# Row sums of two attention layers turned by DMA through DRAM instead of on TensorE

## The chip, the cores and the metric

The kernel runs on one core of a Trainium2 chip. A core has five engines with a queue of instructions each: TensorE (PE, matrix products and transposes, results in PSUM), VectorE (DVE), ScalarE (ACT), GpSimd (POOL) and SyncE (SP, which here does nothing but issue DMAs). POOL issues DMAs too. All DMAs of the core run on the same 16 DMA engines. Engines run in parallel, each in its own order, and wait for each other through semaphores. The metric is the device time of one execution in microseconds (us); lower is better.

## What is computed

32 graphs of 512 nodes with 256 features go through four attention layers that share one adjacency matrix (about 6% edges, self edges included). Every layer is followed by a residual sum and a normalisation of each node. Cut to the two layers that the change concerns:

```python
# layer 0: eight heads of 32 features, q.k scores
qkv = einsum('fnc,ck->fnk', x, w_qkv)
scores = einsum('fnhd,fmhd->fhnm', q, k) / sqrt(32)
attn = softmax(where(adj > 0, scores, -1e9), axis=-1)
t = einsum('fhnm,fmhd->fnhd', attn, v).reshape(F, N, C)
x = layernorm(x + t, g1, b1)
x = layernorm(x + relu(x @ w1 + b1_) @ w2 + b2_, g2, b2)

# layer 3: four heads of 64 features, additive scores
q = (h @ W).reshape(B, N, 4, 64)
e = e_src[:, :, None, :] + e_dst[:, None, :, :]
e = where(e >= 0, e, 0.2 * e)
attn = softmax(where(adj > 0, e, -9e15), axis=2)
out = elu(einsum('bijh,bjhd->bihd', attn, q))
```

Layers 1 and 2 are single-head attention with other scores. After each layer comes `x = layernorm(x + layer(x))`.

## The kernel before

**Tiling.** A graph's 512 nodes are four chunks (NC = 4) of 128 partitions; the 256 features are two chunks (KC = 2). All numbers are float32. Exponentials of scores are held transposed: in a tile `p` the partitions are the attended nodes m, the free axis the attending nodes n. The softmax is not normalised there: the product of exponentials and values and the sum of exponentials are formed apart, and the product is divided at the end.

**Layers 0 and 3.** For layer 0, `exps` forms scores of four heads at once on four row groups of PE (L1034) and ACT takes exponentials (L1038). DVE masks with the adjacency matrix (L1086, one operation of 128x2048). PE multiplies by the values into `oT`, features by nodes (L1093). The sums over m are also taken with DMAs: POOL issues accumulating DMAs `p<-p` (`add_dma`, L972), which add up the tiles of four chunks; SP joins two halves (L1112); then four products with a picking matrix (L1065, in `sums`) leave the sums of the eight heads in a PSUM bank, one row of 512 nodes per head, at partitions 32j and 32j + 1. In layer 3, DVE builds the exponentials as a maximum of two products (L1290) and masks them (L1297), PE multiplies by the values (L1306) and takes the sums of four heads (L1281), at partitions 32j. For the last graph (`at_once`) PE takes all sums itself and no accumulating DMA is used.

**The step that changes** is in `sums_back`, `rinv0` and `rinv3`. The sums lie with nodes along the free axis; they are wanted with nodes on partitions. ACT copies the bank to a tile `e` (`evac`, L890), PE transposes its four 128x128 blocks with the identity (L985), and DVE takes reciprocals of the few useful columns straight from PSUM (L994 for layer 0, L1002 for layer 3) into a small tile `ri`. `heads_out` transposes `oT` back, nodes on partitions, in two groups of four (L1017), and DVE scales each group by the reciprocals (L1020). In layer 0 two range checks of the reciprocals follow (L1045, L1046).

**Order.** There is no fixed loop order in the program. Every step is handed to a planner (`plan(engine, ns, run, reads, writes, ...)`) with an engine, a duration, what it reads and writes, and a `lag`: time after the issue of a DMA until its data are taken to have landed. The planner (`place`) walks a model of time and puts the instructions of up to six graphs (WAYS) into each engine's queue by due times. A due time is PACE times the number of the graph plus a place in a table (TENTHS, with tables of their own for the first graphs, FIRST, and the last, LAST); START holds the first graphs back, and EARLY says how far ahead of its due time a step may be placed. On the chip the queues run in the order so made; the waits are on real events. So a step whose true duration differs from the planner's makes its engine wait, or leaves slack.

**Buffers** are of fixed kinds (KINDS): 8 PSUM banks, 8 tiles `p`, 4 tiles `e`, 3 tiles `ri` and others. A step that needs a buffer is placed when one is free.

**SP's queue** holds, for each graph, the load of x (L1347), the store of the result (L1354), the half sum of layer 0 (L1112), and for the additive layers 1 and 3 a row through DRAM: `row<-gT` (L1186) writes it and L1192 reads it back to all partitions, as tile `G`, on which DVE's L1211 and L1290 depend.

Of the kernel before, what the change touches and what calls it, by code (L numbers as in the profile page):

```python
# [9 lines left out]
FP = mybir.dt.float32  # L10
# [7 lines left out]
P = 128  # L18
# [8 lines left out]
H0, H3 = 8, 4  # L27


WAYS = 6  # L30
PACE = 81.87
STAY = 0.00
START = (0, 10.17, 59.24, 97.18, 85.64)
EARLY = 186.52

TENTHS = (0, 35.72, 65.32, 68.92, 152.58, 202.32, 246.27, 266.73, 356.34, 362.66, 490.49)
FIRST = (
    (0, 35.72, 65.32, 62.35, 138.44, 202.98, 246.27, 266.73, 356.34, 362.66, 490.49),
    (-28.44, 35.72, 73.98, 55.02, 197, 202.32, 246.27, 266.73, 356.34, 362.66, 490.49),
    (-31.13, 30.72, 65.32, 68.92, 152.58, 202.32, 246.27, 266.73, 356.34, 362.66, 490.49),  # L40
    (0, 35.77, 65.37, 68.97, 152.63, 202.32, 246.27, 266.73, 356.34, 362.66, 490.49),)
LAST = (
    (0, 35.72, 65.32, 68.92, 152.58, 202.32, 246.27, 266.73, 354.73, 363.36, 490.49),
    (0, 35.72, 65.32, 68.92, 152.58, 202.32, 246.27, 266.73, 356.34, 362.66, 490.49),
    (0, 35.72, 65.32, 68.92, 152.58, 202.26, 246.21, 266.73, 356.34, 412.91, 557.81),
    (-0.21, 35.51, 65.11, 68.71, 152.37, 202.11, 226.96, 232.14, 316.44, 341.17, 500.04),
    (-6.23, 29.49, 59.09, 8.93, 61.49, 76.67, 155.18, 191.54, 257.43, 316.36, 394.47),)
@with_exitstack
def general_path(
    ctx: ExitStack,  # L50
# [387 lines left out]
PE, DVE, ACT, POOL, SP, DMA = "PE", "DVE", "ACT", "POOL", "SP", "DMA"  # L438
# [191 lines left out]
def fast_path(  # L630
# [34 lines left out]
    nc = tc.nc  # L665
    B, N, C = x.shape
    NC = N // P
    KC = C // P
# [4 lines left out]
    dram = ctx.enter_context(tc.tile_pool(name="dram", bufs=1, space=DRAM))  # L673
# [4 lines left out]
        "x": (6, [P, NC, C]), "y": (7, [P, NC, C]), "v": (3, [P, NC, C + 2 * H3]),  # L678
        "t": (9, [P, KC, N]), "p": (8, [P, 4, N]), "e": (4, [P, N]),
        "st": (6, [P, NC, 6]), "mv": (6, [P, NC, 2]), "rs": (18, [P, NC]),  # L680
        "e1": (6, [P, NC * H3]), "gs": (2, [P, NC * H3]), "ri": (3, [P, NC * H0]),
        "gT": (2, [NC * H3, P]),
    }
    buffers = {kind: [const.tile(shape, FP, name=f"{kind}_{i}") for i in range(n)]
               for kind, (n, shape) in KINDS.items()}
    buffers["bank"] = [psum.tile([P, N], FP, name=f"bank_{i}") for i in range(8)]
    buffers["row"] = [dram.tile([NC * H3, P], FP, name=f"row_{i}") for i in range(4)]


    nc.scalar.preload_act_table_set("natural_log_exp_and_others")  # L690
    ident = const.tile([P, P], FP, name="ident")
# [21 lines left out]
    plan = Plan({kind: len(tiles) for kind, tiles in buffers.items()})  # L713
# [7 lines left out]
    def T(slot):  # L721
        return slot.tile if slot.kind is None else buffers[slot.kind][slot.index]
# [4 lines left out]
    def dve(ns, run, reads, writes, port=False):  # L727
        plan(DVE, ns, run, reads, writes, port)
# [159 lines left out]
    def evac(dst, to, src, frm, n, writes):  # L888

        act(170 + n * 0.84, lambda: nc.scalar.activation(to(T(dst)), frm(T(src)), AF.Copy),  # L890
            [src], writes)
# [83 lines left out]
        plan(POOL, 950, run, reads, [dst, started])  # L975
        plan(DMA, 5600 if src else 2650, None, reads + [started], [dst], lag=2500)

    def sums_back(sm):

        sT, bank = Slot("e"), Slot("bank")  # L980
        evac(sT, lambda t: t, sm, lambda b: b, N, [sT])

        def run():
            for c in range(NC):
                nc.tensor.transpose(T(bank)[:, c * P:(c + 1) * P],  # L985
                                    T(sT)[:, c * P:(c + 1) * P], ident)
        plan(PE, 440, run, [sT], [bank])
        return bank

    def rinv0(sm):  # L990


        bank, rinv = sums_back(sm), Slot("ri")
        dve(360, lambda: nc.vector.reciprocal(  # L994
            T(rinv)[:, :NC * H0].rearrange("p (c g j) -> p c g j", c=NC, g=KC),
            T(bank).rearrange("p (c j r) -> p c r j", c=NC, j=4)[:, :, 0:KC, :]), [bank], [rinv])
        return rinv

    def rinv3(sm):

        bank, rinv = sums_back(sm), Slot("ri")
        dve(250, lambda: nc.vector.reciprocal(  # L1002
            T(rinv)[:, :NC * H3], T(bank).rearrange("p (s r) -> p s r", r=32)[:, :, 0]),
            [bank], [rinv])
        return rinv

    def heads_out(oT, rinv, heads):
# [45 lines left out]
    def layer0(xs, at_once):  # L1053
# [7 lines left out]
        oT, sm, totals = Slot("t"), Slot("bank"), []  # L1061
# [19 lines left out]
        for g in range(KC):  # L1081
            av, ps = Slot("bank"), []
            for m in range(NC):
                p = Slot("p")
# [21 lines left out]
        else:  # L1106
# [5 lines left out]
            plan(SP, 450, lambda: nc.sync.dma_start(T(low)[64:], T(high)[64:]), totals, [low, started])  # L1112
            plan(DMA, 1300, None, totals + [started], [low], lag=2500)
            plan(PE, 870, lambda: sums(2, low, True, True), [low], [sm], tiling=2)
        rinv = rinv0(sm)
        t = heads_out(oT, rinv, H0)

        dve(370, lambda: within(T(rinv)[:, :NC * H0], R_MIN, R_MAX), [rinv], [], True)
# [12 lines left out]
        for d in range(KC):  # L1131
            bank = Slot("bank")
# [8 lines left out]
        f = Slot("y")  # L1141
        for c0 in range(0, NC, 2):
            bank = Slot("bank")
# [129 lines left out]
    def layer3(xs, at_once):  # L1273
        xT = transposed(xs)
        totals = []
        q, G, oT, sm = Slot("v"), Slot("p"), Slot("t"), Slot("bank")
        project(xT, l3w, 0, C + 2 * H3, q)
        e1, e02 = gates(q, H3, G)

        def sums(h, p, part, start, stop):  # L1280
            nc.tensor.matmul(T(sm)[32 * h:32 * h + 32, :], pick[:, 0, :], T(p)[:, part, :],  # L1281
                             start=start, stop=stop)
        for k in range(KC):
            av = Slot("bank")
            for m0 in range(0, NC, 2):
                p = Slot("p")
                for m in range(2):
                    for i in range(2):
                        def run(p=p, m=m, i=i, h=2 * k + i, r=(m0 + m) * H3 + 2 * k + i):
                            nc.vector.tensor_scalar(T(p)[:, 2 * m + i, :], T(G)[:, h, :],  # L1290
                                                    T(e1)[:, r:r + 1], T(e02)[:, r:r + 1],
                                                    ALU.mult, ALU.max)
                        dve(560, run, [G, e1, e02], [(p, 2 * m + i)], True)

                def masked(p=p, m0=m0):
                    p4 = T(p).rearrange("p (m h) n -> p m h n", m=2)
                    nc.vector.tensor_tensor(  # L1297
                        p4, p4, T(edge_t)[:, m0:m0 + 2, :].unsqueeze(2).to_broadcast([P, 2, 2, N]),
                        ALU.mult)
                dve(2300, masked, [p, edge_t], [p], True)  # L1300

                def run(p=p, m0=m0, k=k, av=av):
                    for m in range(2):
                        for i in range(2):
                            h = 2 * k + i
                            nc.tensor.matmul(T(av)[i * D3:(i + 1) * D3, :],  # L1306
                                             T(q)[:, m0 + m, 2 * H3 + h * D3:2 * H3 + (h + 1) * D3],
                                             T(p)[:, 2 * m + i, :], start=(m0 + m == 0),
                                             stop=(m0 + m == NC - 1))
                plan(PE, 1770, run, [q, p], [av], tiling=3)  # L1310
                if at_once:
                    plan(PE, 1740, lambda p=p, k=k, m0=m0: [sums(
                        2 * k + i, p, 2 * m + i, m0 + m == 0, m0 + m == NC - 1)
                        for m in range(2) for i in range(2)], [p], [sm], tiling=2)
                    skip(2 if m0 else 0)
                elif m0 == 0:
                    total = p
                else:
                    add_dma(total, p)
                    add_dma(total, None)  # L1320
                    totals.append(total)
            evac(oT, lambda t, k=k: t[:, k, :], av, lambda b: b, N, [(oT, k)])
        if at_once:
            skip(1)
        else:
            plan(PE, 870, lambda: [sums(h, totals[h // 2], h % 2, True, True) for h in range(H3)],
                 totals, [sm], tiling=2)
        t = heads_out(oT, rinv3(sm), H3)

        e, y = Slot("y"), Slot("y")  # L1330
        for c0 in range(0, NC, 2):
            w, parts = slice(c0, c0 + 2), (c0, c0 + 1)
            act(600, lambda w=w: nc.scalar.activation(T(e)[:, w, :], T(t)[:, w, :], AF.Exp),
                [(t, c) for c in parts], [(e, c) for c in parts])
            act(600, lambda w=w: nc.scalar.activation(T(y)[:, w, :], T(t)[:, w, :], AF.Relu),
                [(t, c) for c in parts], [(y, c) for c in parts])
            add(y, y, xs, c0)
            dve(790, lambda w=w: nc.vector.scalar_tensor_tensor(
                T(y)[:, w, :], T(e)[:, w, :], 1.0, T(y)[:, w, :], ALU.min, ALU.add),
                [(s, c) for s in (y, e) for c in parts], [(y, c) for c in parts], True)  # L1340
        return y
# [95 lines left out]
```

## Time and profile before

| | |
|---|---|
| Median of 3 runs | 2897.5 us (2895.68 to 2899.0) |
| Profiled execution: time, span | 2893.58 us, 2891.7 us |
| PE clock granted | 0.993 |
| Chain that ended last | PE 92%, DVE 3%, DMA 2% of the span |
| DMA queues, share of 16 engines' span | POOL's p<-p 57.2%, SP's 11.6% |
| DVE masking of layer 0, L1086 | 256 operations, 618.2 us |
| PE output transposes L1017 | 512, 68.8 us |

The page counts, for each engine, the time in which an instruction of it ran. The share is an average: filling and draining of the pipeline of graphs are in it. In a line of a group, the numbers are the count, the busy time, the mean of one in ns, and after the last bar the idle time of the engine ahead of these instructions and what ended it. A matrix product in float32 appears as two records of PE, a transpose as one. DMA packets are counted one by one with their size.

### The profile page before, as it was taken

What the parts mean: (1) busy time and instruction counts of PE and PEld (TensorE: products, weight loads), DVE (VectorE), ACT (ScalarE), POOL (GpSimd) and SP (SyncE); (2) the same over time, 40 slices, a digit from 0 to 9 for tenths busy, and PEclk for the clock granted to TensorE, in tenths of its full rate; (3) what the DMA queues carried; (4) which work ended last, traced back from release to release, by engine and by line L of the source; (5) the groups of instructions that cost most, each with busy time, mean ns of one, the idle gap of its engine ahead of it and who ended that gap; (6) DMA issues with size and microseconds to landing.
All of it is one profiled execution on the core that took longest, in us unless ns stands there. A gap on an engine that the chain in (4) does not pass through costs nothing.

```text
span 2891.7 us, 39629 instructions
## 1 busy us (share of the span) xinstructions
PE 2832.4 (98%) x14014; PEld 1579.2 (55%) x14014; DVE 2443.2 (84%) x4076; ACT 1885.5 (65%) x4104; POOL 865.9 (30%) x962
## 2 busy tenths in 40 slices
PE   8899999999999999999999999999999999999996
PEld 3355555555555555555555555555555555554562
DVE  5568888888888988888988888988888888888877
ACT  4566667666667666666666666666676666676553
POOL 1233333232333232332232333232333323333312
PEclk9999999999999999999999999999999999999998
DMA  6856777777777777777777777776776777775125
GB/s 168 169 110 142 150 159 164 154 144 160 145 161 153 159 149 158 149 160 157 147 152 150 157 157 155 152 160 144 162 157 150 155 153 146 161 163 115 35 55 132
DMA packets 101149, 424.44 MB, mean 147 GB/s; under 512 B 10256, under 2 KB 46224, under 8 KB 59152
## 3 DMA queue, kind: packets, MB, share of 16 engines
q0 software_dynamic: 49600, 325.08, 57.2%
q1 hardware_dynamic: 51344, 96.75, 11.6%
q8 instruction: 113, 1.85, 0.2%
q14 instruction: 92, 0.75, 0.1%
HBM read 63.38 MB, written 17.10 MB: 28 GB/s over the span
## 4 chain that ended last, share of the span: by engine, by line
PE 92%; DVE 3%; DMA 2%; issue 1%; ACT 1%; POOL 0%; SPq 0%; ACTq 0%; DVEq 0%; POOLq 0%
PE bank L929 15%; PE bank L915 11%; PE bank L1034 9%; PE bank L1093 8%; PE bank L1306 8%; PE bank L1221 7%; PE bank L1244 7%; PE bank L1260 7%; PE bank L902 5%; PE bank L1136 4%; PE bank L1148 4%; PE bank L1017 2%; DMA p<-p 1%; PE bank L1281 1%; PE bank L1065 1%
## 5 line engine op out<-in xcount | busy, mean ns | idle before, releaser
L972 POOL DMA_DIRECT2D p<-p x372 | 322.3, 871 | 1787.8 <-DMA p<-p 568.4
L1086 DVE TENSOR_TENSOR p<-p,edge_t 128x2048 f32<-128x2048 f32 x256 | 618.2, 2424 | 59.7 <-ACT p L1038 59.5
L890 ACT ACTIVATE t<-bank 128x512 f32<-128x512 f32 x640 | 373.5, 596 | 384.2 <-PE bank L915 125.4
L1038 ACT ACTIVATE p<-bank 128x512 f32<-128x512 f32 x1024 | 537.9, 599 | 89.2 <-PE bank L1034 87.6
L943 DVE BATCH_NORM_STATS2 st<-y 128x6 f32<-128x256 f32 x768 | 315.9, 411 | 35.6 <-POOL y L960 26.0
L1290 DVE TENSOR_SCALAR p<-p,e,e 128x512 f32<-128x512 f32 x512 | 331.3, 680 | 1.0 <-DMA p<-row 1.0
L960 POOL TENSOR_TENSOR y<-y,x 128x512 f32<-128x512 f32 x192 | 273.7, 1432 | 158.2 <-ACT y L1265 100.1
L1297 DVE TENSOR_TENSOR p<-p,edge_t 128x2048 f32<-128x2048 f32 x128 | 304.9, 2382 | 2.2
L1034 PE MATMUL bank<-t,t 32*128 32x512 f32 x2048 | 302.6, 644 | 0.0
L953 ACT ACTIVATE x<-y,rs,rs 128x256 f32<-128x256 f32 x512 | 277.6, 596 | 24.6 <-DVE rs L950 24.3
L1093 PE MATMUL bank<-p,v 128*32 128x512 f32 x2048 | 275.2, 609 | 12.5 <-DVE p L1086 9.7
L1306 PE MATMUL bank<-p,v 128*64 128x512 f32 x1024 | 242.8, 605 | 3.6 <-DVE p L1297 3.6
L915 PE MATMUL bank<-t,wqkv 128*128 128x512 f32 x512 | 241.6, 595 | 0.7 <-ACT t L890 0.7
L1221 PE MATMUL bank<-v,p 128*128 128x257 f32 x1024 | 237.8, 381 | 0.7 <-DVE p L1214 0.4
L890 ACT ACTIVATE v<-bank 128x264 f32<-128x264 f32 (+2 forms) x384 | 176.5, 460 | 90.2 <-PE bank L929 88.3
L1260 PE MATMUL bank<-v,p 128*128 128x257 f32 x1024 | 227.4, 380 | 0.0
L1244 PE MATMUL bank<-t,t 128*128 128x512 f32 x512 | 225.1, 592 | 0.0
L1221 PEld LDWEIGHTS bank<-v,p 128*128 128x128 f32 x1024 | 189.5, 190 | 40.3 <-issue 16.3
L1260 PEld LDWEIGHTS bank<-v,p 128*128 128x128 f32 x1024 | 194.2, 190 | 28.6 <-issue 1.3
L1034 PEld LDWEIGHTS bank<-t,t 32*128 32x128 f32 x2048 | 86.0, 184 | 169.5 <-issue 101.5
L944 DVE BATCH_NORM_AGGREGATE mv<-st 128x2 f32<-128x6 f32 x768 | 139.7, 182 | 26.3
L902 PE MATMUL bank<-ident,x 128*128 128x128 f32 x1024 | 148.9, 279 | 11.7 <-DMA x<-in_x_dram 7.7
(121 smaller groups left out, 4148.8 us busy)
## 6 DMA issues: line engine op xcount, KB each, us to landing
p<-p POOLq DMA_DIRECT2D x248, 1024.0 KB, 7.2
p<-p POOLq DMA_DIRECT2D x124, 512.0 KB, 5.7
p<-row SPq DMA_DIRECT2D x32, 1024.0 KB
x<-in_x_dram SPq DMA_DIRECT2D x32, 512.0 KB
out_dram<-x SPq DMA_DIRECT2D x32, 512.0 KB
p<-p SPq DMA_DIRECT2D x31, 512.0 KB
e<-row SPq DMA_DIRECT2D x32, 256.0 KB
t<-in_adj_dram SPq DMA_DIRECT2D x4, 256.0 KB
```

What stands on the lines that cost most here:

```text
L890: act(170 + n * 0.84, lambda: nc.scalar.activation(to(T(dst)), frm(T(src)), AF.Copy), [src], writes)
L915: nc.tensor.matmul(T(bank), T(w)[:, i, col:col + P], T(xT)[:, i, :], start=(i == 0), stop=(i == KC - 1))
L929: nc.tensor.matmul(T(bank)[:, j * width:(j + 1) * width], T(xT)[:, k, (c0 + j) * P:(c0 + j + 1) * P], T(w)[:, k, col:col + width], start=( ...
L1034: nc.tensor.matmul(T(banks[j]), T(kT)[r, g, m * P:(m + 1) * P], T(qT)[r, g, :], start=True, stop=True)
L1038: act(600, lambda j=j: nc.scalar.activation(T(p)[:, j, :], T(banks[j]), AF.Exp, scale=1.0 / math.sqrt(D0)), [banks[j]], [(p, j)])
L1086: dve(2420, lambda p=p, m=m: nc.vector.tensor_tensor(T(p), T(p), T(edge_t)[:, m, :].unsqueeze(1).to_broadcast([P, J, N]), ALU.mult), [p, ( ...
L1093: nc.tensor.matmul(T(av)[j * D0:(j + 1) * D0, :], T(v)[:, m, h * D0:(h + 1) * D0], T(p)[:, j, :], start=(m == 0), stop=(m == NC - 1))
L1221: nc.tensor.matmul(T(bank)[:, :C + 1], T(p)[:, m, c * P:(c + 1) * P], T(v)[:, m, 2:C + 3], start=(m == 0), stop=(m == NC - 1))
L1244: nc.tensor.matmul(T(bank), T(xT)[:, k, m * P:(m + 1) * P], T(qT)[:, k, :], start=(k == 0), stop=(k == KC - 1))
L1260: nc.tensor.matmul(T(bank)[:, :C + 1], T(p)[:, m, c * P:(c + 1) * P], T(v)[:, m, :C + 1], start=(m == 0), stop=(m == NC - 1))
L1290: nc.vector.tensor_scalar(T(p)[:, 2 * m + i, :], T(G)[:, h, :], T(e1)[:, r:r + 1], T(e02)[:, r:r + 1], ALU.mult, ALU.max)
L1306: nc.tensor.matmul(T(av)[i * D3:(i + 1) * D3, :], T(q)[:, m0 + m, 2 * H3 + h * D3:2 * H3 + (h + 1) * D3], T(p)[:, 2 * m + i, :], start=(m0 ...
```

## The change

The transposes on PE are replaced by a way through DRAM. A new function `rinv_of` serves both layers. After the same copy on ACT, four DMAs on SP write the useful rows (two per j in layer 0, one in layer 3) to a DRAM buffer `line`, 2 KB each row. When all four have landed, one more DMA on SP reads the buffer so that nodes lie on partitions: element (h, c, p) goes to partition p, column (h, c). Runs in DRAM and in SBUF do not match in that access, so it moves in pieces of 4 bytes, 4096 of them in layer 0 and 2048 in layer 3. DVE then takes reciprocals from this tile, reordered to what `heads_out` reads. The planner's numbers for the new steps are 450 ns for each issue, and lags of 2000 ns for a write and 3500 ns for the read. A fourth `ri` tile and four `line` buffers are added. The constants of the due times are others (PACE, START, EARLY and the three tables).

```diff
-PACE = 81.87
+PACE = 83.15
-START = (0, 10.17, 59.24, 97.18, 85.64)
-EARLY = 186.52
+START = (0, 11.15, 69.71, 99.02, 152.63)
+EARLY = 180.50
...
-    def sums_back(sm):
-        sT, bank = Slot("e"), Slot("bank")
-        evac(sT, lambda t: t, sm, lambda b: b, N, [sT])
-        def run():
-            for c in range(NC):
-                nc.tensor.transpose(T(bank)[:, c * P:(c + 1) * P],
-                                    T(sT)[:, c * P:(c + 1) * P], ident)
-        plan(PE, 440, run, [sT], [bank])
-        return bank
-
-    def rinv0(sm):
...
-    def rinv3(sm):
...
+    def rinv_of(sm, heads):
+        sT, line, raw, rinv = Slot("e"), Slot("line"), Slot("ri"), Slot("ri")
+        G, R = heads // 4, NC * heads
+        evac(sT, lambda t: t, sm, lambda b: b, N, [sT])
+        for j in range(4):
+            plan(SP, 450, lambda j=j: nc.sync.dma_start(
+                T(line)[:heads, :].rearrange("(g j) n -> j g n", j=4)[j], T(sT)[32 * j:32 * j + G, :]), [sT], [(line, j)], lag=2000)
+        def back():
+            with nc.allow_non_contiguous_dma(reason="a transpose of few elements"):
+                nc.sync.dma_start(T(raw)[:, :R], T(line)[:heads, :].rearrange("h (c p) -> p (h c)", p=P))
+        plan(SP, 450, back, [(line, j) for j in range(4)], [raw], lag=3500)
+        dve(200, lambda: nc.vector.reciprocal(
+            T(rinv)[:, :R].rearrange("p (c g j) -> p g j c", c=NC, g=G),
+            T(raw)[:, :R].rearrange("p (g j c) -> p g j c", g=G, j=4)), [raw], [rinv])
         return rinv
...
-        rinv = rinv0(sm)
+        rinv = rinv_of(sm, H0)
...
-        t = heads_out(oT, rinv3(sm), H3)
+        t = heads_out(oT, rinv_of(sm, H3), H3)
```

In the changed kernel the lines are: line writes L986, reading back L991, reciprocals L993, output transposes L1008, scaling L1011, exponentials' scores of layer 0 L1025, masking of layer 0 L1077 and of layer 3 L1288, the half sum L1103, products of layer 0 L1084, of layer 1 L1212, of layer 2 L1251, of layer 3 L1297, projections L930, the row's transpose L1173, normalisation L951.

## The prediction

> **What bounds the kernel now.** I read the page's totals first, then the stretches, the waits of TensorE, the groups that the diff touches, and last the DMA queues.
>
> ```profile
> span 2891.7 us, 39629 instructions
> PE 2832.4 (98%) x14014; PEld 1579.2 (55%) x14014; DVE 2443.2 (84%) x4076; ACT 1885.5 (65%) x4104; POOL 865.9 (30%) x962
> ```
>
> TensorE (PE) is idle for 59 us of the whole span. The stretches (columns: start:end, length, then busy time of PE, PEld, DVE, ACT, POOL, the clock, the DMA share, GB/s) say where:
>
> ```profile
> 60.00:150.00 90.00, 79.56 (x408) 33.78 (x400) 50.74 (x66) 52.43 (x105) 27.85 (x27) 0.94 0.85 170
> 800.00:1500.00 700.00, 698.83 (x3489) 392.62 (x3488) 617.76 (x1007) 471.10 (x1028) 213.73 (x241) 1.00 0.73 154
> 2800.00:2891.00 91.00, 66.40 (x291) 31.11 (x289) 66.64 (x128) 38.34 (x85) 21.52 (x21) 0.88 0.49 111
> ```
>
> In the middle PE has 1.2 us idle in 700, while DVE has 82 us, about 10 us for each graph (one graph per 87.2 us, the spacing of the x loads). Only filling and draining leave PE room. So PE time saved in the middle shows in full, as long as nothing else comes to hold PE up.
>
> The groups concerned:
>
> ```profile
> L985 PE MATMUL bank<-ident,e 128*128 128x128 f32 x256 | 40.8, 282 | 2.0 <-ACT e L890 1.9
> L994 DVE RECIPROCAL ri<-bank 128x32 f32<-128x32 f32 x32 | 11.4, 357 | 34.2 <-PE bank L985 34.2
> L1002 DVE RECIPROCAL ri<-bank 128x16 f32<-128x16 f32 x32 | 8.0, 250 | 0.2 <-PE bank L985 0.2
> L890 ACT ACTIVATE e<-bank 128x512 f32<-128x512 f32 x64 | 39.0, 610 | 60.2 <-PE bank L1065 46.3 <-PE bank L1281 13.9
> ```
>
> The transposes cost PE 40.8 us. DVE already waits 34 us for them and PE does not suffer: of small DVE waits much is absorbed.
>
> [...] three column loads at the start (1 KB each) moved as 4-byte packets. From 9 to 10 us:
>
> ```profile
> DMA packets 1031, 0.23 MB, mean 230 GB/s; under 512 B 810, under 2 KB 1031, under 8 KB 1031
> q1 hardware_dynamic: 1031, 0.23, 120.0%
> ```
>
> The 221 larger ones are of 1 KB. From 5.5 to 6.2 us 252 such packets filled the 16 engines: 16 x 0.7 / 252 = 44 ns of an engine each. 221 of them take 9.8 of the 16 engine-us, which leaves at most 7.7 ns for each of the 810 small ones; the packet records say 9 ns, and I use 9. [...] the trace has 0.92 to 0.96 us from issue to first packet where the engines were idle, and I use 0.92. [...]
>
> ```profile
> 1410.99 0.39 SPq L1354 DMA_DIRECT2D out_dram<-x  x1
> DMA packets 96, 0.79 MB, mean 197 GB/s; under 512 B 0, under 2 KB 0, under 8 KB 0
> q0 software_dynamic: 95, 0.78, 97.8%
> ```
>
> The store was issued at 1410.99, and up to 1415 us only packets of POOL's p<-p moved: the store's first came at 1415.02, after that transfer had drained. So a DMA of SP waits for the p<-p in flight. p<-p holds 57% of the engines' time (queue q0), in bursts of 5.6 us on average; a DMA that falls at random waits 0.57 x 2.8 = 1.6 us, 4.5 us at worst.
>
> **The change part by part.** *Removed:* 256 transposes, 40.8 us on PE. Their weight loads overlap matmuls. A PSUM bank is held for less; I give that nothing. *DVE:* 19.4 us of reciprocals from PSUM go; 64 from SBUF come, at about 0.2 us (the 128x32 operation L1045 took 207 ns): 7 us less, hidden, since DVE has idle time. The copy on ACT stays.
>
> *Added:* 320 DMAs on SP at 0.27 to 0.38 us, about 100 us of an engine that now mostly waits (L1112 alone 1486.8 us). 4096 pieces for layer 0 and 2048 for layer 3 are 256 and 128 for each engine, 2.3 and 1.15 us at 9 ns; over 32 graphs 110 us, 3.8% of the span on top of a share near 70%. p<-p gets later by up to 2.3 us at a time; PE waited for p<-p only 3.5 us in all (L1065 and L1281), so I give that nothing.
>
> *The new chain,* from the end of the sums: copy on ACT 0.7 and signal 0.1; four writes of a line, 0.3 apart, the last landing 1.25 after its start (the writes row<-gT at L1186 have 1.23 to 1.29 to the start of the dependent read): reading back is issued at 0.8 + 0.9 + 1.25 = 3.0. Then 0.92, 2.3 (1.15) of pieces, 0.4 for completion (what is left of the 1.25 after the 0.73 to its first packet and the packets): 6.6 us in layer 0, 5.4 in layer 3. Two waits behind p<-p, 1.6 each, make 9.8 and 8.6.
>
> *The room for it:* in the order of the changed program's instructions, between the sums of layer 0 and its output transposes L1008 PE has in the middle of the run 8 products of L1251 (0.444 each by the groups of before), 8 of L930 (0.484), 4 of L1025 (0.296), one L1173 (0.275) and 8 of L1297 (0.474): 12.7 us, times 0.94 for the overlap between groups (PE's groups sum to 3011, the union is 2832) 11.9. In layer 3 it is 11.8 the same way. DVE comes to the reciprocal L993 before it scales the output: ahead by 3.4 us in layer 0 (two range checks, L951, a product L1077 of 2.4), by 2.2 in layer 3. So DVE stands at L993 about 8.9 and 10.0 us after the sums. On average the chain overshoots by 0.9 us in layer 0 and not in layer 3; with the spread of the p<-p waits I take 2 us per graph. Behind the waiting L993 are all later DVE operations, among them the masked products that PE waits for. Of DVE's 10 us per graph the 2 are mostly absorbed; 10% leaking is 6 us in all. Bounds: 0, and, if none is absorbed, 62.
>
> *SP's queue:* behind layer 3's reading back stands the half-sum L1103, which now has 48 us of waiting per graph; ahead of layer 0's stands the store, which waits for ACT (6 us per graph now at L1354): counted in the spread. Behind it stand the next load and the rows of G; DVE waited 28.6 us for these (L1211, L1290), so each could add about 1 us; absorbed likewise.
>
> *The ends:* in the drain the last graph's chain is bare. Before, 2.9 us lay between the copy (to 2871.80) and the scaling (2874.72); after it is 2.1 + 0.92 + 1.15 + 0.4 = 4.6, plus 1.7 for the store put in front and some 2 for what that store waits for: +6, and 1 for the graph before it: +7. In the fill the first graph's chain grows by about 6; others fill in part: +4 (0 to 8).
>
> *The new constants* reorder all engines. Nothing measured prices this: between -10 and +10; I take 0.
>
> *Sum:* 2891.7 - 40.8 + 6 + 7 + 4 = 2868. The runs' median lies 5.8 above the profiled span, so 2874.
>
> **The rivals.** *A, slower: the 4-byte reading drains slowly.* One mechanism: DVE waiting at L993. The 9 ns come from loads that were queued up before; a single DMA alone is seen no faster than a store's 512 packets in 1.7 us, 300 per us. At that rate layer 0 takes 13.6 us instead of 2.3, and DVE stands for 12 + 4 us per graph against 10 idle; at 600 per us it is 4.5 + 1 more, 7.5 with the 2, and half of that absorbed leaves 3.5 x 31 = 110 us: 2868 - 6 + 110 = 2972. It decides from a leak of 1 us per graph (40.8 less 11 for the ends, over 31): about 4 us of drain in layer 0, if of the 4 us of waiting that this makes a quarter leaks. A middle case is 2935. For it: no row shows 4096 pieces in one DMA. Against: 810 small packets in 1 us beside others.
>
> *B, no change: PE's gain is taken by the order.* The waits absorb less, a third leaks (21 us instead of 6), and the new order costs 10: 2868 + 15 + 10 = 2893, 2899 as a run. For it: DVE is 88% busy in the middle. Against: PE waits for DVE's products only 13 us in all.
>
> *C: the transposes are not on the path.* Against: PE stands in the chain for 92%, and its 1.2 us of idle in 700.
>
> **How the numbers follow.** Forecast 0.63 (own range 2856 to 2889), A 0.25, B 0.10, C within B, better than 2856 0.02. 80% reaches from 2852 to 2932, which leaves out the upper half of A. A difference of 0.2% (5.8 us) is what can be told from none: faster 0.65, same 0.10, slower 0.25.
>
> **What would show it.** Right: PE busy near 2792, idle in the middle still under 1%, L993 waiting under 3 us per graph, reading back done 4 us after issue in layer 0. Wrong: L993 with over 5 us a time, PE waiting for L1077 or L1288, DMA packets of 4 bytes much longer than 9 ns, or more than 20 us added to the drain.

## The result, and the profile after

| | before | after |
|---|---|---|
| Median of 3 runs | 2897.5 us | 2946.9 us (2944.95 to 2948.43) |
| Ratio, 95% interval | | 1.017 (1.0147 to 1.0193) |
| Span of the profiled execution | 2891.7 us | 2943.2 us |
| First store of a result issued at | 363.7 us | 400.6 us |
| Spacing of the stores, graphs 8 to 24 | 87.29 us | 87.34 us |
| From the store of graph 24 to the last store | 426.7 us | 436.1 us |

The change made the kernel 49 us slower; 2874 was predicted. In the profiled executions 43 of the 51 us are lost by the store of graph 8 (1061.8 us before, 1104.6 after), 0.7 between graphs 8 and 24, and 9.5 from there to the last store: in the middle what is gained and what is lost cancel. The page of after, totals and the chain that ended last:

```profile
span 2943.2 us, 39669 instructions
PE 2824.9 (96%) x13758; PEld 1553.4 (53%) x13758; DVE 2317.5 (79%) x4076; ACT 1891.0 (64%) x4104; POOL 995.8 (34%) x962
...
PE 81%; DMA 12%; DVE 3%; ACT 2%; SPq 1%; issue 1%; POOL 0%; ACTq 0%; DVEq 0%; POOLq 0%
```

PE is busy for 7.5 us less than before, not 40.8, and is idle for 118 us instead of 59. DMA has gone from 2% of the chain to 12%, 11 of them in `ri<-line` and `line<-e`, the new way through DRAM. Where PE is idle (busy time of PE, PEld, DVE, ACT, POOL by stretch, then the clock, the DMA share, GB/s); the first line is before's, the others are after's:

```profile
150.00:400.00 250.00, 246.73 (x1216) 139.50 (x1215) 193.74 (x337) 162.05 (x360) 81.07 (x86) 0.99 0.67 140
60.00:150.00 90.00, 68.46 (x336) 28.71 (x336) 36.43 (x35) 40.59 (x79) 23.22 (x21) 0.89 0.82 155
150.00:400.00 250.00, 229.19 (x1097) 130.26 (x1090) 187.17 (x328) 153.74 (x335) 72.50 (x77) 0.96 0.64 126
800.00:1500.00 700.00, 692.25 (x3397) 382.12 (x3395) 568.62 (x997) 468.54 (x1018) 255.68 (x240) 1.00 0.77 154
```

The fill lost most: before, PE was busy for 79.56 us of the stretch from 60 to 150 us and for 246.73 of the next 250; now for 68.46 and 229.19. In the middle it stands still for 7.75 us in 700, about 1 us per graph, where it stood still for 1.2 in all. The reciprocals, and then PE's own waits (total, times, longest):

```profile
L993 DVE RECIPROCAL ri<-ri 128x16 f32<-128x16 f32 (+1 forms) x64 | 18.7, 292 | 96.4 <-DMA ri<-line 96.4
```

```profile
PE bank L1084 <- DVE p L1077: 33.1, 14, 11.3
PE bank L903 <- DVE y L1218: 21.2, 23, 2.9
```

DVE waits 96.4 us for the data that are read back, and PE waits for DVE: up to 11.3 us at a time for masked exponentials (L1077), and 23 times for L1218, about once per graph. L1218 writes the result of layer 1, which L903 transposes next. Neither uses the reciprocals; both stand behind L993 in DVE's queue.

**In the fill.** Graph 1, layer 0, in order of time (start, length, then in brackets the idle time ahead of the instruction and what ended it):

```profile
154.16 2.14 SPq L986 DMA_DIRECT2D line<-e  x4
161.38 0.38 SPq L991 DMA_DIRECT2D ri<-line  x1
175.30 0.36 DVE L993 RECIPROCAL ri<-ri 128x32 f32<-128x32 f32 x1 [12.76 <-DMA ri<-line]
176.03 2.28 DVE L1077 TENSOR_TENSOR p<-p,edge_t 128x2048 f32<-128x2048 f32 x1
178.37 1.94 PE L1084 MATMUL bank<-p,v 128*32 128x512 f32 x8 [11.25 <-DVE p L1077]
```

The reading back is issued at 161.38, and L993 runs at 175.30. What the engines moved meanwhile, from 162.4 to 174.8:

```profile
DMA packets 4487, 2.21 MB, mean 178 GB/s; under 512 B 4143, under 2 KB 4230, under 8 KB 4230
q0 software_dynamic: 288, 2.10, 81.6%
q1 hardware_dynamic: 4198, 0.11, 21.2%
```

The reading's 4096 pieces began at 162.40 and ended at 174.80; in the packet records 256 packets of 8 KB of p<-p (10.07 us of each engine's time) lie between them. They are not spread evenly. The same view from 162.4 to 164.2 us, while the pieces have the engines for themselves, and from 165 to 174 us, while p<-p is there:

```profile
q1 hardware_dynamic: 2641, 0.01, 72.8%
...
DMA packets 499, 1.92 MB, mean 213 GB/s; under 512 B 265, under 2 KB 265, under 8 KB 265
q0 software_dynamic: 249, 1.91, 102.2%
q1 hardware_dynamic: 249, 0.00, 4.0%
```

In 1.8 us 2641 pieces move. Then p<-p comes, and in the next 9 us only 249 pieces move beside 233 packets of 8 KB: the two queues take turns, one piece of 4 bytes for each packet of 0.63 us. The last 733 pieces follow within 0.8 us, after 174.0, when the p<-p is done.

**In the middle.** The same steps in layer 3 of a graph at 1045 us, with what follows on DVE and PE:

```profile
1045.68 1.76 SPq L986 DMA_DIRECT2D line<-e  x4
1050.89 0.39 SPq L991 DMA_DIRECT2D ri<-line  x1
1057.98 0.26 DVE L993 RECIPROCAL ri<-ri 128x16 f32<-128x16 f32 x1 [2.66 <-DMA ri<-line]
1058.29 0.48 DVE L1218 SCALAR_TENSOR_TENSOR y<-bank,rs,x 128x256 f32<-128x256 f32 x1
1058.83 0.66 PE L903 MATMUL bank<-ident,y 128*128 128x128 f32 x4 [0.92 <-DVE y L1218]
```

The four lines are issued by 1047.44, and only 3.4 us later have they landed and the reading back is issued (in layer 0 1.3 us later); the 2048 pieces took 0.9 us once they moved; yet L993 runs 7.1 us after L991. Both are longer than the plan's lags (2.0 and 3.5), so L993 stands too early in DVE's queue. Between 1051 and 1056.3 the engines moved:

```profile
DMA packets 142, 1.03 MB, mean 195 GB/s; under 512 B 16, under 2 KB 16, under 8 KB 16
q0 software_dynamic: 126, 1.03, 102.1%
```

One p<-p of 1 MB, queued just before (POOL issued it at 1049.55), holds all 16 engines; the first piece comes 4.76 us after the issue, when 112 of that p<-p's 128 packets have started. For these 112 packets no turns were taken. So it is in layer 3 of nearly every graph: first piece after 4.54 us in the median (layer 0: 2.11, behind the store of another graph, or 1.02 with nothing ahead). Then DVE's wait of 2.66 us becomes 0.92 us of PE. Without the wait L1218 would have ended at 1056.1; PE had work up to 1057.9 anyhow. So 1.74 us of this wait cost nothing, and all beyond does. Two other graphs, with a longer and a shorter wait:

```profile
881.13 0.26 DVE L993 RECIPROCAL ri<-ri 128x16 f32<-128x16 f32 x1 [3.90 <-DMA ri<-line]
881.99 0.66 PE L903 MATMUL bank<-ident,y 128*128 128x128 f32 x4 [2.16 <-DVE y L1218]
...
1582.76 0.26 DVE L993 RECIPROCAL ri<-ri 128x16 f32<-128x16 f32 x1 [2.08 <-DMA ri<-line]
1583.62 0.66 PE L903 MATMUL bank<-ident,y 128*128 128x128 f32 x4 [0.35 <-DVE y L1218]
```

PE waits for L1218 after 25 of layer 3's reciprocals, and in 24 of them its idle time is DVE's wait less 1.71 to 1.75 us (once less 1.89). The waits average 2.6 us in the middle: about 0.9 us each reach PE, 24.6 us in the 25.

### The profile page after: what moved, and what is told of

Read it like the earlier page. It is cut to its first block, busy times and chain, and to the rows that moved or that the text cites. A ratio compares the mean times of both kernels' runs of the same rounds, so it can differ in the third digit from the quotient of the medians.

```text
span 2943.2 us, 39669 instructions
## 1 busy us (share of the span) xinstructions
PE 2824.9 (96%) x13758; PEld 1553.4 (53%) x13758; DVE 2317.5 (79%) x4076; ACT 1891.0 (64%) x4104; POOL 995.8 (34%) x962
## 4 chain that ended last, share of the span: by engine, by line
PE 81%; DMA 12%; DVE 3%; ACT 2%; SPq 1%; issue 1%; POOL 0%; ACTq 0%; DVEq 0%; POOLq 0%
PE bank L930 15%; PE bank L916 11%; PE bank L1251 8%; PE bank L1297 8%; PE bank L1235 7%; PE bank L1025 7%; DMA ri<-line 7%; PE bank L1084 6%; PE bank L903 5%; PE bank L1127 4%; DMA line<-e 4%; PE bank L1139 4%; PE bank L1212 2%; PE bank L1056 1%; PE bank L1008 1%; PE bank L1272 1%
## 5 line engine op out<-in xcount | busy, mean ns | idle before, releaser
L973 POOL DMA_DIRECT2D p<-p x372 | 331.3, 892 | 1489.9 <-DMA p<-p 476.8
L1077 DVE TENSOR_TENSOR p<-p,edge_t 128x2048 f32<-128x2048 f32 x256 | 597.2, 2334 | 122.8 <-ACT p L1029 122.2
L961 POOL TENSOR_TENSOR y<-y,x 128x512 f32<-128x512 f32 x192 | 346.0, 1852 | 241.5 <-ACT y L1256 180.3
L1281 DVE TENSOR_SCALAR p<-p,e,e 128x512 f32<-128x512 f32 x512 | 337.4, 705 | 3.0 <-DMA p<-row 3.0
L1084 PE MATMUL bank<-p,v 128*32 128x512 f32 x2048 | 276.9, 613 | 33.6 <-DVE p L1077 33.1
L1025 PE MATMUL bank<-t,t 32*128 32x512 f32 x2048 | 299.2, 646 | 7.0 <-DVE y L1011 7.0
L1288 DVE TENSOR_TENSOR p<-p,edge_t 128x2048 f32<-128x2048 f32 x128 | 294.5, 2301 | 3.3
L1251 PE MATMUL bank<-v,p 128*128 128x257 f32 x1024 | 245.5, 386 | 0.0
L1297 PE MATMUL bank<-p,v 128*64 128x512 f32 x1024 | 241.8, 602 | 2.8 <-DVE p L1288 2.8
L1212 PE MATMUL bank<-v,p 128*128 128x257 f32 x1024 | 242.4, 386 | 0.0
L1212 PEld LDWEIGHTS bank<-v,p 128*128 128x128 f32 x1024 | 188.0, 190 | 66.5 <-issue 24.1
L1251 PEld LDWEIGHTS bank<-v,p 128*128 128x128 f32 x1024 | 188.2, 190 | 65.6 <-issue 22.7
L903 PEld LDWEIGHTS bank<-ident,x 128*128 128x128 f32 x1024 | 120.0, 143 | 96.4 <-issue 40.7
L903 PE MATMUL bank<-ident,x 128*128 128x128 f32 x1024 | 150.6, 280 | 14.4 <-ACT x L954 9.5
L1025 PEld LDWEIGHTS bank<-t,t 32*128 32x128 f32 x2048 | 83.6, 185 | 148.0 <-issue 85.3
```

Of the source, the lines that this page charges most:

```text
L903: nc.tensor.transpose(T(bank)[:, (2 * k + c) * P:(2 * k + c + 1) * P], T(src)[:, c0 + c, k * P:(k + 1) * P], ident)
L1025: nc.tensor.matmul(T(banks[j]), T(kT)[r, g, m * P:(m + 1) * P], T(qT)[r, g, :], start=True, stop=True)
L1077: dve(2420, lambda p=p, m=m: nc.vector.tensor_tensor(T(p), T(p), T(edge_t)[:, m, :].unsqueeze(1).to_broadcast([P, J, N]), ALU.mult), [p, ( ...
L1084: nc.tensor.matmul(T(av)[j * D0:(j + 1) * D0, :], T(v)[:, m, h * D0:(h + 1) * D0], T(p)[:, j, :], start=(m == 0), stop=(m == NC - 1))
L1212: nc.tensor.matmul(T(bank)[:, :C + 1], T(p)[:, m, c * P:(c + 1) * P], T(v)[:, m, 2:C + 3], start=(m == 0), stop=(m == NC - 1))
L1251: nc.tensor.matmul(T(bank)[:, :C + 1], T(p)[:, m, c * P:(c + 1) * P], T(v)[:, m, :C + 1], start=(m == 0), stop=(m == NC - 1))
```

## Experiments

Each ratio below is against runs of before on the same chip. Line numbers in variants are shifted by a few lines.

### Is it the wait, the traffic, or the pieces?

Three variants of after. The first takes every reciprocal from a constant, with all DMAs still made; the second also leaves out the DMAs; the third reads `line` back in 128 contiguous runs: the same number of bytes, with the transposition left out. The first two leave out the true row sums.

```diff
 e1_nowait and e2_nodma:
-            T(rinv)[:, :R].rearrange("p (c g j) -> p g j c", c=NC, g=G),
-            T(raw)[:, :R].rearrange("p (g j c) -> p g j c", g=G, j=4)), [raw], [rinv])
+            T(rinv)[:, :R], nominal.to_broadcast([P, R])), [raw], [rinv])
 e2_nodma besides: no dma_start at L986 and L991
 e3_contiguous:
-                nc.sync.dma_start(T(raw)[:, :R], T(line)[:heads, :].rearrange("h (c p) -> p (h c)", p=P))
+                nc.sync.dma_start(T(raw)[:, :R], T(line)[:heads, :].rearrange("h n -> (h n)").rearrange("(p r) -> p r", p=P))
```

> The changed kernel, but the reciprocals L993 are taken from a constant (32) instead of the tile read back from DRAM; all five DMAs are still issued and every engine keeps its order. Left out: the use of the true row sums, so the output is scaled wrongly. Theory W (DVE's wait for the read-back costs the time: 24 us in the first two graphs, about 2.6 us per graph later of which PE loses about 1): 2885 to 2905. Theory O (the new order of the engines costs it): 2935 to 2950. Theory D (the added DMA traffic slows the other transfers): 2935 to 2950.

> As the run with the constant, and the five DMAs are not issued either; same order on PE, DVE, ACT and POOL. Left out: as there, and the way through DRAM. Theory W: as the run with the constant, within 5 us. Theory D: at least 20 us faster than the run with the constant. Theory O: 2935 to 2950.

> The changed kernel, but the buffer is read back in its own order: 128 pieces of 128 or 64 bytes instead of 4096 or 2048 of 4 bytes. Left out: the transposition, so the nodes get reciprocals of others. Same orders. If the 4-byte pieces are what makes the wait: 2890 to 2915. If the wait comes from the DMAs standing behind p<-p (line writes and read): 2930 to 2945. Theory O: 2940 to 2950.

Measured: without the wait 2889.2 us (0.9971, 0.9964 to 0.9978); without the DMAs too 2888.2 (0.9968, 0.9957 to 0.998); with contiguous reading 2900.5 (1.0012, 1.0002 to 1.0021). So waiting at L993 costs 58 us; the 320 DMAs and their 200,000 packets cost about 1 us, which is within the noise; and 46 of the 58 hang on the 4-byte pieces. That last reading needs care: alone the pieces drain no slower than predicted (below). In the third variant DVE still waits,

```profile
DVE ri L993 <- DMA ri<-line: 45.5, 28, 8.9
```

but in the middle mostly for less than the 1.74 us that are free (1.16, 0.74, 1.35, with some of 2.4): the stores are 86.48 us apart, against 86.30 without the wait and 87.34 in after. Cutting 1 us off a wait that stands 1 us over these 1.74 recovers nearly all. Of the 26 reciprocals of layer 3 that wait here, PE stands still for L1218 only behind the four that wait 2.0 us and more, for the wait less 1.7 to 1.9. In the fill the gain is another: graph 1's reading of 128 runs is over when the p<-p comes, DVE waits 0.47 us in place of 12.76, and the first store is issued at 385.2 us instead of 400.6.

### Which wait: layer 0 or 3, middle or fill?

```diff
+        if heads == H3:            # e5_nowait_layer3;  e6_nowait_first2: if the graph is 0 or 1
+            dve(200, lambda: nc.vector.reciprocal(T(rinv)[:, :R], nominal.to_broadcast([P, R])), [raw], [rinv])
+            return rinv
```

> After, but the reciprocals of layer 3 are taken from a constant: its row sums are copied, written and read back as before, and nothing waits for them. Layer 0 is as in after, and the order of the instructions is that of after. Theory W3 (in the steady part the wait at L993 is layer 3's, because its lines and its reading back stand behind p<-p; in the fill it is that of layer 0 of the first two graphs): the spacing of graphs falls from 87.7 us to about 86.5, 1.2 x 29 = 35 us, and the fill's 24 us stay: 2912 us. Rival W0 (my prediction: the wait is that of layer 0, whose 4096 pieces drain for twice as long as layer 3's 2048): hardly anything changes, 2940 or more.

> After, but in graphs 0 and 1 alone the reciprocals of layers 0 and 3 are taken from a constant; the DMAs run all the same and the order is that of after. Theory W3 (24 of the 58 us of waiting are lost while the pipeline fills, where no other graph covers the way through DRAM): 2947 - 24 = 2923 us, the spacing of graphs in the middle stays at 87.7. Rival F (filling costs only what I predicted, 4 us, and all the rest is lost in the middle): 2943.

Measured: 2912.5 us (1.0043, 1.0026 to 1.006) and 2921.7 (1.008, 1.0064 to 1.0097), where W3 said 2912 and 2923. Against after's 2946.9 that is 34 and 25 us: together the whole of the wait (layer 3's wait of graph 1, 4.2 us, is in both). PE in the fill and in the middle, first without layer 3's waits, then without those of graphs 0 and 1:

```profile
60.00:150.00 90.00, 68.44 (x332) 28.76 (x336) 36.61 (x34) 40.88 (x80) 23.20 (x21) 0.89 0.82 155
800.00:1500.00 700.00, 700.00 (x3440) 387.62 (x3439) 587.83 (x1019) 475.31 (x1028) 258.31 (x243) 1.00 0.78 156
```

```profile
60.00:150.00 90.00, 73.83 (x376) 28.53 (x368) 45.45 (x52) 48.23 (x96) 26.09 (x22) 0.92 0.87 164
800.00:1500.00 700.00, 691.86 (x3396) 381.35 (x3395) 568.07 (x993) 470.01 (x1022) 255.44 (x240) 1.00 0.77 154
```

The one fills the middle wholly and leaves the fill as it was; the other gives back a part of the fill and leaves the middle. The two losses are separate.

### Is it the length of the wait, or what stands behind it?

In after's plan, layer 3's reciprocals of graphs 2 to 31 and what depends on them are held back for 3 us of the plan's time; only DVE's queue comes out different, L993 moving behind five instructions, L1218 among them. Graphs 0 and 1 stay as they are, though the expectation speaks of every graph. It computes all that after does.

```diff
+        turned.hold = 0 if plan.graph < 2 else 3000 if heads == H3 else 0      # turned: the step L993
...
+        if op.hold or any(used & {(s.kind, s.index) for s in o.slots} for o in self.late):
+            self.late.append(op)                      # put out 3 us of the plan later
+            return
```

> After, whole in what it computes, with one thing changed in the order: in every graph the reciprocals L993 of layer 3 stand five DVE instructions later, behind L1217, L1218, L944, L945 and one L1281 (1.7 us together), just ahead of the scaling that uses them. All other queues are as in after. Theory S (TensorE loses time only where L1218, which hands back a bank, stands behind the waiting L993; a wait that stands ahead of nothing TensorE needs soon costs nothing): about 0.9 us of the mean wait of 2.6 remains and doesn't show; the spacing of graphs falls to 86.5 as without the wait, 2912 us. Rival P (the loss goes with the length of DVE's wait): 0.9/2.6 of 35 us remain, 2924 us.

Measured: 2917.9 us (1.0071, 1.0054 to 1.0087), 29 of the 34 us back. The stores are 86.32 us apart, as without the wait at all. DVE's wait at the reciprocals, in the same view as above:

```profile
DVE ri L1016 <- DMA ri<-line: 35.8, 12, 12.7
```

23.0 of the 35.8 us are those of layer 0 in graphs 0 and 1 (10.29 and 12.71); all others together are ten waits and 12.8 us. The 2917.9 lies midway between S's 2912 and P's 2924; the spacing decides for S: five small instructions moved, 1.7 us of work, gave back in the middle what removing the wait did. (The expectation says L1218 hands back a bank; what the trace has L903 wait for is the tile `y` that L1218 writes.) The 5 us that remain against 2912.5 lie outside graphs 8 to 24; 2.4 of them are PE's idle time behind graph 1's reciprocals of layer 3, which were not moved and wait 4.1 us.

### What were the transposes worth?

Before with each row-sum transpose done twice; before with none, reciprocals from a constant, its order unchanged; and before with the due-time constants of after and nothing else.

```diff
 e7_transposes_twice:
+                for _ in range(2):
                     nc.tensor.transpose(T(bank)[:, c * P:(c + 1) * P],
 e9_before_no_transposes: the four transposes are left out
 e4_before_newconst: PACE, START, EARLY, TENTHS, FIRST, LAST as in after
```

> Before, with every transpose of the row sums done twice into the same place, 256 more of 128x128 on TensorE, and nothing else changed. Theory S (a transpose costs on the path its share of the spacing between graphs, where taking the eight away gave 0.94 us per graph): 2898 + 0.94 x 32 = +30, 2928 us. Rival B (it costs its busy time, 8 x 159 ns = 1.27 us per graph, as I predicted): +41, 2939 us. If DVE's slack hides a part: less than +20.

> Before, without the 256 transposes of row sums; the reciprocals of layers 0 and 3 are taken from a constant, the copy on ScalarE remains, and the order of everything else is that of before. It measures the gain that the prediction started from, without the changed order. Busy time (my prediction): 40.8 us less, 2858. By what it cost to do the transposes twice (20 us): 2878. By the spacing of graphs (0.94 us each, from after without the wait against before): 30 less, 2868. Whatever lies between this and the 2889 us of after without the wait is the cost of the new order.

> The kernel before with the new constants of the due times alone. Theory O (constants): 2930 to 2950. Theory W: 2890 to 2915.

Measured: twice 2919.0 us (1.007, 1.0053 to 1.0087), +20; none 2881.4 (0.9941, 0.9924 to 0.9958), -16; the constants on before's steps 3003.8 (1.0371, 1.0354 to 1.0389), +105. The group of the transposes, done twice:

```profile
L986 PE MATMUL bank<-ident,e 128*128 128x128 f32 x512 | 68.2, 276 | 2.1 <-ACT e L890 1.9
```

256 more raise the busy time from 40.8 to 68.2 us, 27.4, or 107 ns each, though each lasts 276 ns from start to end. The records of a row overlap: a group of four is busy for 0.64 us, one of eight for 1.07. By the spacing of stores, adding and removing agree: 88.09 and 86.52 us against 87.29, +0.80 and -0.77 per graph. That is 25 us over 32 graphs; in the variant without transposes the first store comes 6.7 us later (370.4 against 363.7), which takes part of it back. Why, no run here tells.

The constants fit the steps they go with; before's constants on after's steps were not run. What the order as a whole does is seen by comparing the variant without DMAs and wait (2888.2) with before without transposes (2881.4): each against its own runs of before, -10.5 and -15.8, so 5 us for the new order (8 by the two ratios), with an uncertainty as large. It is 0.22 us per graph better in the middle (86.30 against 86.52) and starts later.

**The sum.** Transposes gone -16, new order +5, DMAs +1, wait +58 to 59: +49, as measured (2946.9 - 2897.5). Each step is the difference of two neighbouring variants, so the sum has to close; the wait alone is confirmed apart, by the 34 and 25 us.

### A version that takes the gain and not the wait?

Graphs 0, 1 and 31 are turned on TensorE as before, the others through DRAM with layer 3's reciprocals moved as above; the due times were set anew in two ways. The third has the second's due times, and the reciprocals and their scaling one masking operation later still; ACT's order changes with it.

```diff
+        if plan.graph in (0, 1, 31):          # the four transposes and the reciprocal from PSUM
...
+        turned.hold = 3000                    # graphs 2 to 30, layer 3; e12_mixed_later: 5000
```

> A version meant to beat both. The way through DRAM is kept for graphs 2 to 30, with layer 3's reciprocals five DVE instructions later as in the run with layer 3 later; graphs 0, 1 and 31, whose way through DRAM lies bare while the pipeline fills and drains, are turned on TensorE as in before, with four transposes for each layer. Constants of the due times set anew, slightly. Theory S: 2889 as after without the wait, plus 6 for what was left when only layer 3 was moved, plus 3 x 0.8 for the transposes, less some 4 in the drain: 2893. Rival O (the new order costs more in the fill than the waits did): 2900 or more.

> The same program with another setting of the due times, in which the second graph starts 5 us later. Theory S: 2893 as well; if the two differ by more than 3 us, that is what the order alone is worth.

> The same as the other setting, with layer 3's reciprocals and the scaling that uses them one masking operation of DVE (2.3 us) later still, past the mean wait. Theory S: the waits that are left at the reciprocals vanish and with them up to 6 us: 2887 to 2893. Rival H (held-back scaling keeps two PSUM banks for 2.3 us more and TensorE waits for them): 2895 to 2905.

Measured: 2907.4 us (1.0036, 1.0024 to 1.0048), 2903.0 (1.002, 1.0014 to 1.0027) and 2942.7 (1.0155, 1.0141 to 1.0169). None beats before. The second is 44 us faster than after; its first store comes at 366.3 us, almost as in before, but at the store of graph 8 it is 22 us behind before (1083.8 against 1061.8); the loss stands between the first store and the second (479.1 against 450.7). Rival O's number came true, its reason only in part: the fill is 10 us shorter than with layer 3 later alone, which keeps the fill's waits (1094.3), and 16 us longer than without any wait (1067.9). No run here has longer lags for the new DMAs in the plan. The third shows the other side of moving a step back. In the middle, PE's score products of layer 0, in the second version and the third:

```profile
L1065 PE MATMUL bank<-t,t 32*128 32x512 f32 x2048 | 301.4, 647 | 0.1
```

```profile
L1065 PE MATMUL bank<-t,t 32*128 32x512 f32 x2048 | 324.5, 643 | 9.5 <-DVE y L1051 9.5
```

The scaling (L1051 here) reads the PSUM banks of the output transposes; now that it comes later, these products wait for it, 24 times for about 0.4 us, and their busy time is 23 us longer. The stores go from 86.33 to 87.86 us apart. Rival H's cause is the one that the trace shows; its 2895 to 2905 was far too low.

## Why the prediction was wrong

From the predicted 2874 us to the measured 2947 it is 73. By the runs about 41 of them are waiting (58, where leak, fill and drain together had 17), 25 the transposes (16 gained, where the sum had 40.8), 5 the new order and 1 the traffic. Leak, fill or transposes, each put right alone, would have taken the predicted gain of 24 us nearly or wholly away; it takes all of them to make 49 us of loss.

**The step that failed is the leak,** and with it two more, the fill and the price of the transposes. The prediction found the place (L993), the size of the waits (2 us per graph; 72 us over 29 graphs, 2.5, after the first two) and the queue behind it, and then let a tenth through, 6 us. By the run without layer 3's waits, 34 of its 69 us of waiting came out as time (DVE's wait at the reciprocals is 27.0 us in that variant, 96.4 in after). 24.6 of them are the idle times ahead of L1218's users; where the rest goes is not resolved. The tenth was read off before, where DVE waited 34 us for the transposes (L994, 1.1 us a time) and PE did not suffer. But what hides a wait here is a slack per wait, 1.74 us at this place, not a share: 2.6 shows by 0.9. What the slack at L994 was in before, no run measured; 1.1 us was hidden there. The 34 lie below the bound of "none is absorbed", 62.

**The fill** was put at +4 (0 to 8); it is 25. The chain of the first two graphs took 17.3 and 23.7 us from the sums to the reciprocals. The prediction had SP's transfers wait for a p<-p in flight and then move alone. In truth the first piece waits for what is queued ahead (4.54 us from the issue in the median of layer 3, 1.02 with nothing ahead), and in graph 1 the p<-p that came during the reading took turns with it, one packet of 0.63 us for each piece; the reading, 2.1 us in the middle, took 12.4. And with two graphs in the pipeline PE has nothing else at hand: it stood idle for 11.25 us.

**Which layer** was wrong. The wait was expected mostly in layer 0, for its 4096 pieces. In the middle layer 0's chain ran as worked out: reading back issued 3.09 us after the sums (3.0), first piece 2.11 us later, pieces 2.2 us (2.3); DVE came to L993 at 9.8 and never waited. Layer 3 has half the pieces and all the wait: in the middle its lines landed 3.4 to 4.5 us after the last issue (layer 0: 1.3 in most graphs), with a p<-p moving meanwhile; and between the issue of its reading and the pieces 85 or more packets of a p<-p moved in 26 of 32 graphs, in layer 0 in graph 0 alone. The prediction had 1.6 us at random for each. In the middle the order repeats with each graph, and an average over a random phase misses such a collision. DVE's arrival was right in layer 3, 10.3 us (10.0), though the room less the work ahead as given is 8.5 and 9.6, not 8.9 and 10.0.

**The transposes** were priced at their busy time, 40.8 us. The factor of 0.94 for the overlap of PE's groups was applied to the room, not here; and for these transposes it is 27.4/40.8 = 0.67. They are worth 25 us by the spacing in the middle, 16 in the end.

**Right:** 9 ns per piece (4096 in 2.1 us: 16 x 2.1 / 4096 = 8.2 ns of an engine each), the added traffic at nothing (1 us), new constants within 10 (5).

**Right by luck: the drain** (+7 predicted, 9.5 from the store of graph 24 on). 4.1 of it are there without any wait, so they belong to the order. The last graph's chain did take 8.0 us from the copy to the scaling, as worked out (8.3), but it takes 7.5 without the wait too, and the last L993 waits only 0.48 us. Of the other 5.3, 3.7 stand already at the next graph's store, behind one wait of 4.74 us at 2553 us.

**The rivals.** The time fell into A's cases (2935 to 2972; half of its 7.5 us is 3.75, which makes 2978), at A's place, but its mechanism is out: 4096 pieces in 2.1 us are 1900 per us, not 300 or 600. In graph 1's fill they do move at 330 per us, but because a p<-p takes turns with them. What A had right is that the pieces count, as the microsecond over the 1.74 and as turns. B's mechanism, waits absorbed less than thought and an order that costs, is what happened, at half instead of a third, and with a fill that neither case had.

## What to carry to other kernels

Find for each wait what stands behind it on the same engine and how much slack the bottleneck has at that very place; here, behind layer 3's reciprocals, it was 1.74 us: a wait below it was free, and of the mean wait of 2.6 us the other 0.9 was paid in full. In a schedule that repeats, look up what a new DMA is queued behind, and what will be queued while it moves, at its own time in the cycle. Price the fill and the drain apart: here two graphs in the fill lost 25 us, where little else covered the long way. Price a short TensorE instruction by what one more of it adds to a group (107 ns here), not by the busy time of the group (40.8 us for 256, 159 ns each).

## What the runs showed of the hardware that was not expected

- A single DMA of 4096 pieces of 4 bytes moved in 2.1 us on 16 engines in the median of layer 0, 9 ns a piece in the packet records, as for the queued column loads of before.
- An accumulating packet of 8 KB (0.63 us) and a piece of 4 bytes took turns one for one in the fill: from 165 to 174 us 249 pieces moved beside 233 such packets, where 2641 had moved in the 1.8 us before they came.
- The first piece of the reading came 1.02 us after issue with idle engines, 4.3 to 4.9 in layer 3 in the middle behind a p<-p of 1 MB that POOL queued just before; in one graph 112 of its 128 packets had started by then.
- A 128x128 float32 transpose added 107 ns of PE's busy time in a row of eight, and 0.10 us to the spacing of graphs.
